# Normalising attention outputs instead of attention weights in the last block of a four-block cross-attention kernel

## The chip, the cores and the metric

The kernel runs on one core of one Trainium2 chip. The metric is the device time of one execution in microseconds; the time of a kernel is the median of several runs. The profile comes from one further execution, taken by the hardware profiler.

## What is computed

Four transformer blocks are applied one after the other to x of shape (8, 112, 256), with a context of shape (8, 375, 192) that all four share. All is float32. Blocks 0 and 1 have self-attention, cross-attention and a gated feed-forward part with 16 heads of 64; block 2 is one cross-attention with heads of 64. Block 3, which the change touches, has 16 heads of 16:

```python
h = _layernorm(x, ln1_w, ln1_b)
q, k, v = split(h @ qkv_w + qkv_b)                    # 16 heads of 16
attn = softmax(where(causal | tgt_mask, -inf, q @ k.T * scale))
x = x + (attn @ v) @ proj_w + proj_b
h = _layernorm(x, ln2_w, ln2_b)
q = h @ q_w + q_b; k = enc @ k_w + k_b; v = enc @ v_w + v_b
attn = softmax(where(enc_mask, -inf, q @ k.T * scale))
x = x + (attn @ v) @ out_w + out_b
h = _layernorm(x, ln3_w, ln3_b)
x = x + gelu(h @ mlp1_w + mlp1_b) @ mlp2_w + mlp2_b
```

A softmax divides each row of exponentials by its sum. The division is by a number for each query and head, so it can be done on the weights or on the product of the weights with v.

## The kernel before

**Stages and tiles.** The ten stages 0 to 9 are self, cross, feed-forward for blocks 0 and 1, one cross for block 2, and self (7), cross (8), feed-forward (9) for block 3. The 896 rows of x lie in seven tiles of 128 rows. The attention outputs of a stage go to `oT`, which holds channels on the partitions and all rows along the free dimension. In block 3 every head's 16 channels are padded to 32, so that four heads fill 128 partitions and the 16 heads fill four chunks of `oT`.

**Steps.** An attention stage is cut into steps (`add_step`). In stage 7 a step is one batch with all 16 heads in two blocks of eight; in stage 8 it is a quarter of a batch, four heads in two blocks of two. Each step has three parts:

- S (`emit_s`): the score matmuls (L818), then `softmax` for each block: on DVE the mask (L777, stage 7 only), the negated maximum (L783) and a guard for fully masked rows (L787); on ACT one exponential for each head, which also accumulates the sum (L793); then the division. With more than one chunk of keys (stage 8, 375 keys) each head has a reciprocal on DVE (L799) and a multiply on POOL (L800); with one chunk (stage 7, 112 keys) a block has one reciprocal (L803) and one multiply (L804).
- T (`emit_t`): TensorE transposes of the weights into a PSUM tile (L837) and a copy to SBUF (`wT`).
- PV (`emit_pv`): the matmuls of the values with `wT` (L857) and a copy to `oT`.

PSUM copies go through `evac`, which picks ACT (L303, L299) or DVE (L311, L307) by an estimate of each engine's load. The four `mm` PSUM tiles serve all but the scores; the scores have two tiles of their own.

**Around the steps.** The output products of a stage (`add_products`, L549) take, for each of the seven row tiles, a few matmuls of `oT` with the output weights, add to x on DVE (L553), and start the next LayerNorm (`norm`): statistics on DVE (L498, L500, L502), then on POOL a power (L504), the normalised tile xn (L506) and the bias row added to x (L507). `add_norm_transposes` turns xn by TensorE (L520) into `hT`. The values of block 3 are made in `add_self_values` (L605) and `add_context_values` (L728) and spread by `spread_values` (a POOL memset, L624, and a DVE add of the bias row, L625). Two constant tiles `rvs` hold those bias rows.

**What sets the order.** TensorE's order is the order in which the program is emitted. A planner (`Plan`) emits it: in each round the score part of step i+2, the PV part of step i, and the T parts of step i+1, with filler items between (projections, keys, values, products, transposes). An item has a cost in us, a deadline counted in steps, the keys that it needs, and for each of these a gap that must have passed in the planner's own time. `ready` takes the item with the earliest deadline among those whose gaps are over; `pace` spreads fillers over the steps up to their deadlines. The other engines' orders are chosen by the scheduler of the framework and are in-order once chosen. The weights come through a ring of seven slots on SP's DMA queue (`add_load`).

Of the kernel before, what the change touches and what calls it, by code (L numbers as in the profile page):

```python
# [17 lines left out]
H = 16  # L18
# [44 lines left out]
def last_batch(t):  # L63
    return min(B - 1, (P * (t + 1) - 1) // T)
# [198 lines left out]
def kernel(ctx: ExitStack, tc: tile.TileContext, a: dict, out: bass.AP):  # L263
# [19 lines left out]
        return ps_m.tile([P, 512], F32, tag="mm", name="mm")  # L283

    plan = Plan(RINGS)
    load = {"act": 0.0, "dve": 0.0}

    def busy(eng, us):
        load[eng] = max(load[eng], plan.now) + us
# [68 lines left out]
    ctxA = const.tile([KA, B * S], F32, name="ctxA")  # L358
    ctxB = const.tile([2 * KB, B * S], F32, name="ctxB")
    cmask = const.tile([T, B, T], F32, name="cmask")  # L360
    rvs = [const.tile([P, D], F32, name=f"rv{i}") for i in range(2)]

    got = {}

# [74 lines left out]
    def add_ctx_narrow(key, name):  # L439


        def fn():
            t = wpool.tile([P, 2, D], F32, tag="w", name=name)
            nc.gpsimd.memset(t[KB : KB + 1, 1, :], 0.0)
            nc.sync.dma_start(t[:, 0, :], a[name][0:KA, :])
            nc.sync.dma_start(t[:KB, 1, :], a[name][KA:DC, :])
            got[key] = t

        plan.add_load(Item(("load", key), 0, fn, makes=[key]))
# [144 lines left out]

            plan.add(Item(key, 1.5, fn, deadline(j, u), uses=[w], makes=[key], deps=h_deps(st, lo, hi), seg=SEG[st]))

    def add_self_values(st, b, w, deadline, wide, bias=None):
        for hf in range(2 if wide else 1):
            key = ("v", st, b, hf, 0)

            def fn(hf=hf, key=key):
                ps = mm_tile()
                n = 512 if wide else D
                for k in range(2):
                    nc.tensor.matmul(  # L605
                        ps[:T, :n], lhsT=hT[:, k, b * T : (b + 1) * T],
                        rhs=got[w][:, k, hf * 512 : hf * 512 + n], start=(k == 0), stop=(k == 1),
                    )
                t = vpool.tile([P, 512], F32, tag="v", name="v")
                if wide:  # L610
                    evac(t[:T, :], ps[:T, :], n)
                else:
                    spread_values(t, ps, T, bias)
                got[key] = t

            plan.add(
                Item(key, 1.75 if wide else 0.9, fn, deadline(b, hf), uses=[w], makes=[key],
                     deps=h_deps(st, b * T, (b + 1) * T), seg=SEG[st])
            )
# [98 lines left out]
    def ctx_deps(b):  # L718
        return [(("ctxT", b), 4.0)]

    def add_context_values(st, b, w, deadline, bias):
        for c, (k0, kl) in enumerate(KCH):
            key = ("v", st, b, 0, c)

            def fn(k0=k0, kl=kl, key=key):
                ps = mm_tile()
                for k, (ct, rows) in enumerate(((ctxA, KA), (ctxB, KB + 1))):
                    nc.tensor.matmul(  # L728
                        ps[:kl, :D], lhsT=ct[:rows, b * S + k0 : b * S + k0 + kl],
                        rhs=got[w][:rows, k, :], start=(k == 0), stop=(k == 1),  # L730
                    )
                t = vpool.tile([P, 512], F32, tag="v", name="v")
                spread_values(t, ps, kl, bias)
                got[key] = t

            plan.add(Item(key, 0.9, fn, deadline(b), uses=[w], makes=[key],
                          deps=ctx_deps(b) + [(("put", 0), 5.0)], seg=SEG[st]))
# [20 lines left out]


    steps = []  # L760

    def add_step(st, b, blocks, dh, nk, qs, ks, qap, kap, vtile, masked, guard, opos, ochunk):

# [8 lines left out]
        def softmax(blk, ps):  # L772
            ns = len(blk) // 2
            sv = ps[:, :, : ns * nk].rearrange("p b (s k) -> p b s k", k=nk)
            pr = ppool.tile([T, 2, ns, nk], F32, tag="pr", name="pr")
            if masked:
                nc.vector.tensor_add(  # L777
                    pr, sv, cmask[:, b, :].unsqueeze(1).unsqueeze(1).to_broadcast([T, 2, ns, nk])
                )
                sv = pr  # L780
                busy("dve", 1.1)
            nm = small.tile([T, 2, 4], F32, tag="nm", name="nm")
            nc.vector.tensor_reduce(nm[:, :, :ns], sv, AX.X, ALU.max, negate=True)  # L783
            busy("dve", 0.16 + 0.00104 * 2 * ns * nk)
            if guard:

                nc.vector.tensor_scalar_min(nm[:, :, :ns], nm[:, :, :ns], -0.01 * NEG)  # L787
                busy("dve", 0.16)
            sums = small.tile([T, 2, 4], F32, tag="sums", name="sums")
            rinv = small.tile([T, 2, 4], F32, tag="rinv", name="rinv")  # L790
            for n in range(len(blk)):
                bk, sl = n % 2, n // 2
                nc.scalar.activation(  # L793
                    pr[:, bk, sl, :], sv[:, bk, sl, :], AF.Exp, bias=nm[:, bk, sl : sl + 1],
                    accum_out=sums[:, bk, sl : sl + 1],
                )
                busy("act", 0.46 + 0.00084 * nk)
                if nch > 1:
                    nc.vector.reciprocal(rinv[:, bk, sl : sl + 1], sums[:, bk, sl : sl + 1])  # L799
                    nc.gpsimd.tensor_scalar_mul(pr[:, bk, sl, :], pr[:, bk, sl, :], rinv[:, bk, sl : sl + 1])  # L800
                    busy("dve", 0.16)
            if nch == 1:
                nc.vector.reciprocal(rinv[:, :, :ns], sums[:, :, :ns])  # L803
                nc.gpsimd.tensor_tensor(  # L804
                    pr, pr, rinv[:, :, :ns].unsqueeze(3).to_broadcast([T, 2, ns, nk]), ALU.mult
                )
                busy("dve", 0.16)
            return pr

        def emit_s():  # L810
            tiles = [ps_s.tile([T, 2, 512], F32, tag="s", name="s") for _ in blocks]

            order = [(i, n) for i, blk in enumerate(blocks) for n in range(len(blk))]
            if dh == 16:
                order.sort(key=lambda e: (e[1] // 2, e[0]))
            for i, n in order:
                h = blocks[i][n]
                nc.tensor.matmul(  # L818
                    tiles[i][:, n % 2, (n // 2) * nk : (n // 2 + 1) * nk], lhsT=qap(h), rhs=kap(h),
                    start=True, stop=True,  # L820
                )
            for i, blk in enumerate(blocks):
                pr = softmax(blk, tiles[i])
                for n, h in enumerate(blk):
                    cell[h] = pr[:, n % 2, n // 2, :]
# [52 lines left out]
                 deps=[(("T", s, i), 0) for i in range(len(banks))]), False  # L878
        )
        steps.append(len(banks))  # L880

    def self_steps(st, dh):
        first = len(steps)
# [64 lines left out]
    def after_pv(first, per):  # L948

        return lambda t: [(("PV", first + per * (last_batch(t) + 1) - 1), 1.2)]  # L950

    def q_deadline(first, per, j):
        return first + per * 2 * j - 3.4

# [9 lines left out]


    info = []
    SEG = [0, 0, 0, 1, 1, 1, 2, 2, 2, 2]
    for kind, dh in (
        ("self", 64), ("cross", 64), ("ff", 0), ("self", 64), ("cross", 64), ("ff", 0),
        ("cross", 64), ("self", 16), ("cross", 16), ("ff", 0),  # L970
# [21 lines left out]
    def self_stage(st, names, wq, wk, wv, wo):  # L992
# [7 lines left out]
            add_pair_projection(st, "k", j, wk, us, dl, None,  # L1000
                                (lambda m: bcols[:, 8 + m : 9 + m]) if L3 else None)
        for b in range(B):
            add_self_values(st, b, wv, lambda b, hf: first + per * b + hf - 1.3, not L3, rvs[0])

    def cross_stage(st, wq, wk, wv, qscale, vscale):
        kind, first, per, dh = info[st]
# [4 lines left out]
        for b in range(B):  # L1011
            if L3:
                add_context_keys(st, b, wk, 4, lambda b, m: first + 4 * b + m - 3.2, lambda m: bcols[:, 12 + m : 13 + m])
                add_context_values(st, b, wv, lambda b: first + 4 * b - 1.3, rvs[1])
            else:

                add_key_jobs(st, b, wk, lambda b, u: first + 4 * b + u - 3.0)
                add_value_jobs(st, b, wv, lambda b, i: first + 4 * b + (0, 0, 2)[i] - 1.5 + 0.1 * i, vscale)
# [42 lines left out]
    def w(name):  # L1061
        return ("w", name)
# [53 lines left out]
    add_masks()  # L1116
    L3 = "L3_xattn_"

    def add_rvs():
        def fn():  # L1120
            nc.sync.dma_start(rvs[0], a["v_row"].to_broadcast([P, D]))
            r = ROWS.index(L3 + "v_b")
            nc.sync.dma_start(rvs[1], a["rows"][r : r + 1, :].to_broadcast([P, D]))

        plan.add_load(Item(("load", "rvs"), 0, fn))

    add_rvs()
    add_padded(w("q3"), L3 + "qkv_w", slice(0, D))
    add_padded(w("k3"), L3 + "qkv_w", slice(D, 2 * D))
    add_w(w("v3"), L3 + "qkv_w", slice(2 * D, 3 * D))  # L1130
    add_row(("row", 7), L3 + "proj_b")
    add_padded_rows(w("o3"), L3 + "proj_w")
    add_padded(w("qc"), L3 + "q_w", None)
# [11 lines left out]
    add_products(6, 7, w(L + "Wo"), 8, after_pv(f6, 4), norm_by(7))  # L1145
    add_norm_transposes(7, L3 + "ln1_w", L3 + "ln1_b", hT_by(7))
    self_stage(7, None, w("q3"), w("k3"), w("v3"), w("o3"))
    add_products(7, 8, w("o3"), 4, after_pv(f7, 1), norm_by(8))
    add_norm_transposes(8, L3 + "ln2_w", L3 + "ln2_b", hT_by(8))
    cross_stage(8, w("qc"), w("kc"), w("vc"), 0.25, None)  # L1150
    add_products(8, 9, w("oc"), 4, after_pv(f8, 4), norm_by(9))
    add_norm_transposes(9, L3 + "ln3_w", L3 + "ln3_b", hT_by(9))
    ff_stage(9, None, w("m1"), L3 + "mlp1_b", AF.Gelu, f9 - 1)
    add_products(9, None, w("m2"), 8, after_ff(9), lambda t: f9 + 1 + 0.1 * t)
# [74 lines left out]
```

## Time and profile before

| what | value |
|---|---|
| median of 3 runs | 1757.38 us (1756.21 to 1757.7) |
| profiled execution | 1756.8 us, of which 1755.0 us are the span from first to last instruction |
| mean granted TensorE clock | 0.995 |
| PE busy | 1696.6 us |
| POOL busy | 906.6 us |
| DVE busy | 874.6 us |
| ACT busy | 756.1 us |
| block 3: stage 7 from about | 1400 us |
| block 3: stage 8 | from about 1480 to 1702 us |
| block 3: feed-forward, last output | to 1755 us |

PE is the matrix unit of TensorE, PEld its weight loads, DVE the vector engine, ACT the scalar engine, POOL the GpSimd engine. In a row of a group, `x128 | 155.8, 1235` means 128 instructions, 155.8 us busy in all, 1235 ns each; behind the next bar stands the idle time of the engine just ahead of them, and who ended it. A matmul's mean overlaps with its neighbours', so that its cost in a row is the busy time divided by the count. In the table of stretches, the two columns behind the engines are the granted TensorE clock and the DMA engines' busy share.

### The profile page before, as it was taken

To read this page: it belongs to the slowest core of one execution; us is meant where nothing else is said; L and a number is where in the kernel's file an instruction comes from. 1 tells how busy PE (TensorE), PEld (TensorE's weight loads), DVE (VectorE), ACT (ScalarE), POOL (GpSimd) and SP (SyncE) were. 2 spreads that over 40 slices of the span, in tenths; PEclk is the share of its full clock that TensorE was granted. 3 is DMA by queue.
4 is the path that set the end of the run, shared out by engine and by line. 5 is a ranking of instruction groups with operands and counts; after the bars stand their busy time and mean duration, and the time that the engine had idled before them with its cause. 6 is when DMAs were issued, how large, how long until landed. Compare 5 with 4: busy or idle time off the path is not lost.

```text
span 1755.0 us, 30348 instructions
## 1 busy us (share of the span) xinstructions
PE 1696.6 (97%) x11886; PEld 1186.7 (68%) x11886; DVE 874.6 (50%) x2046; ACT 756.1 (43%) x2410; POOL 906.6 (52%) x825
## 2 busy tenths in 40 slices
PE   5999999999999999999999999999999998999989
PEld 4877766666658887666666656666666876666656
DVE  1454454555522444554555522445555588666740
ACT  2553443444521544434444431444444366555641
POOL 4223455566702322655466612645566845888880
PEclk9999999999999999999999999999999999999999
DMA  5011011000101101000000101100000101000000
GB/s 176 11 48 53 3 29 54 25 1 1 49 27 43 28 10 40 25 28 1 25 1 1 43 28 9 10 1 1 7 1 7 12 9 55 1 1 2 1 1 22
DMA packets 39464, 39.12 MB, mean 22 GB/s; under 512 B 16928, under 2 KB 34568, under 8 KB 39321
## 3 DMA queue, kind: packets, MB, share of 16 engines
q1 hardware_dynamic: 39257, 37.13, 7.6%
q8 instruction: 94, 1.54, 0.4%
q14 instruction: 49, 0.40, 0.1%
q0 software_dynamic: 64, 0.05, 0.0%
HBM read 35.48 MB, written 0.92 MB: 21 GB/s over the span
## 4 chain that ended last, share of the span: by engine, by line
PE 85%; POOL 6%; ACT 4%; DVE 4%; issue 1%; DMA 0%; SPq 0%; ACTq 0%; POOLq 0%; DVEq 0%
PE mm L581 11%; PE mm L549 11%; PE mm L837 9%; PE s L818 9%; PE mm L857 9%; PE mm L677 7%; PE mm L643 7%; PE mm L1030 7%; PE mm L686 4%; PE mm L652 4%; POOL pr L800 4%; PE mm L605 3%; ACT pr L793 3%; DVE nm L783 2%; POOL xn L506 1%; PE mm L728 1%
## 5 line engine op out<-in xcount | busy, mean ns | idle before, releaser
L800 POOL TENSOR_SCALAR pr<-pr,rinv 112x375 f32<-112x375 f32 x512 | 623.5, 1236 | 366.2 <-DVE rinv L799 362.8
L793 ACT ACTIVATE pr<-s,nm 112x375 f32<-112x375 f32 (+1 forms) x768 | 373.5, 501 | 240.4 <-DVE nm L783 166.6
L783 DVE TENSOR_REDUCE nm<-s 112x2 f32<-112x750 f32 (+1 forms) x288 | 266.2, 953 | 68.3 <-PE s L818 63.9
L837 PE MATMUL mm<-ident,pr 112*128 112x112 f32 (+2 forms) x1920 | 241.3, 265 | 13.1 <-POOL pr L800 5.2
L837 PEld LDWEIGHTS mm<-ident,pr 112*128 112x128 f32 (+2 forms) x1920 | 214.5, 152 | 58.3 <-issue 15.5
L303 ACT COPY wT<-mm 128x448 f32<-128x448 f32 (+2 forms) x285 | 150.1, 534 | 190.5 <-PE mm L837 190.2
L857 PEld LDWEIGHTS mm<-wT,v 128*64 128x64 f32 (+5 forms) x3840 | 160.3, 129 | 84.6 <-issue 32.5
L804 POOL TENSOR_TENSOR pr<-pr,rinv 112x896 f32<-112x896 f32 x48 | 80.8, 1683 | 253.7 <-DVE rinv L803 228.1
L818 PE MATMUL s<-kT,qT 64*112 64x375 f32 (+3 forms) x1792 | 207.6, 392 | 0.0
L857 PE MATMUL mm<-wT,v 128*64 128x112 f32 (+5 forms) x3840 | 200.1, 264 | 7.4 <-ACT wT L303 4.5
L818 PEld LDWEIGHTS s<-kT,qT 64*112 64x112 f32 (+1 forms) x1792 | 113.1, 172 | 68.2 <-issue 15.3
L793 ACT ACTIVATION_READ_ACCUMULATOR pr<-s,nm 112x1 f32 x768 | 158.0, 206 | 0.0
L799 DVE RECIPROCAL rinv<-sums 112x1 f32<-112x1 f32 x512 | 83.4, 163 | 98.7 <-ACT pr L793 88.1
L311 DVE COPY kT<-mm 128x375 f32<-128x375 f32 (+1 forms) x117 | 65.5, 560 | 133.4 <-PE mm L652 114.4
L311 DVE COPY wT<-mm 128x448 f32<-128x448 f32 (+2 forms) x195 | 118.6, 612 | 21.3 <-PE mm L837 18.2
L311 DVE COPY v<-mm 128x512 f32<-128x512 f32 (+2 forms) x75 | 51.8, 691 | 141.2 <-PE mm L686 118.7
L303 ACT COPY kT<-mm 128x375 f32<-128x375 f32 (+1 forms) x107 | 51.1, 478 | 129.0 <-PE mm L652 115.3
L504 POOL TENSOR_TENSOR rs<-ve,mhalf 128x1 f32<-128x1 f32 x70 | 39.4, 564 | 126.1 <-DVE ve L502 123.9
L553 DVE TENSOR_TENSOR x<-mm,x 128x256 f32<-128x256 f32 x70 | 29.5, 422 | 143.2 <-PE mm L549 143.1
L643 PE MATMUL mm<-ctxA,L_xattn_Wk 128*128 128x375 f32 x256 | 91.5, 480 | 0.0
L677 PE MATMUL mm<-L_xattn_Wv,ctxA 128*128 128x512 f32 (+1 forms) x192 | 90.7, 595 | 0.4 <-ACT hT L299 0.4
L506 POOL TENSOR_SCALAR xn<-x,mv,rs 128x256 f32<-128x256 f32 x70 | 85.8, 1226 | 7.7 <-PE mm L520 1.1
(130 smaller groups left out, 2349.4 us busy)
## 6 DMA issues: line engine op xcount, KB each, us to landing
L_xattn_Wq<-in_L_xattn_Wq_dram SPq DMA_DIRECT2D x3, 1024.0 KB, 6.7
L_xattn_Wo<-in_L_xattn_Wo_dram SPq DMA_DIRECT2D x3, 1024.0 KB, 15.9
L_xattn_w_ff<-in_L_xattn_w_ff_dram SPq DMA_DIRECT2D x3, 1024.0 KB, 5.6
L_xattn_Wp<-in_L_xattn_Wp_dram SPq DMA_DIRECT2D x2, 1024.0 KB, 7.5
L_xattn_wq<-in_L_xattn_wq_dram SPq DMA_DIRECT2D x2, 1024.0 KB, 5.0
L_xattn_wo<-in_L_xattn_wo_dram SPq DMA_DIRECT2D x2, 1024.0 KB, 5.7
L_xattn_mlp_w<-in_L_xattn_mlp_w_dram SPq DMA_DIRECT2D x2, 1024.0 KB, 4.9
cn<-in_ctx_dram SPq DMA_DIRECT2D x2, 843.8 KB
```

The lines of the kernel that those rows point to most:

```text
L303: nc.scalar.copy(dst, src)
L311: nc.vector.tensor_copy(dst, src)
L549: nc.tensor.matmul(ps[:, :D], lhsT=oT[:, c, t * P : (t + 1) * P], rhs=got[w][:, c, :], start=(c == 0), stop=(c == n - 1),)
L581: nc.tensor.matmul(ps[:, i * 2 * T : (i + 1) * 2 * T], lhsT=got[w][:, k, m * P : (m + 1) * P], rhs=hT[:, k, lo:hi], start=(k == 0), stop=( ...
L643: nc.tensor.matmul(ps[:, :S], lhsT=got[w][:, (2 * u + i) * P : (2 * u + i + 1) * P], rhs=ctxA[:, cols], start=True, stop=False,)
L677: nc.tensor.matmul(ps[: KCH[c][1], :], lhsT=lhs(ctxA, slice(0, KA), c), rhs=got[w][:, hf * 512 : (hf + 1) * 512], start=True, stop=False,)
L783: nc.vector.tensor_reduce(nm[:, :, :ns], sv, AX.X, ALU.max, negate=True)
L793: nc.scalar.activation(pr[:, bk, sl, :], sv[:, bk, sl, :], AF.Exp, bias=nm[:, bk, sl : sl + 1], accum_out=sums[:, bk, sl : sl + 1],)
L800: nc.gpsimd.tensor_scalar_mul(pr[:, bk, sl, :], pr[:, bk, sl, :], rinv[:, bk, sl : sl + 1])
L818: nc.tensor.matmul(tiles[i][:, n % 2, (n // 2) * nk : (n // 2 + 1) * nk], lhsT=qap(h), rhs=kap(h), start=True, stop=True,)
L837: nc.tensor.transpose(pt[:kl, i * T : (i + 1) * T], cell[h][:, c * P : c * P + kl], ident[:T, :T])
L857: nc.tensor.matmul(po[p0 : p0 + dp, blk * T : (blk + 1) * T], lhsT=got[vk][:kl, hv * dp : (hv + 1) * dp], rhs=wt, start=(c == 0), stop=(c ...
```

## The change

In stages 7 and 8 (`dh == 16`) the weights stay unnormalised: `softmax` returns after the exponentials, whose sums go into one tile `bsums` for each batch, a column for each head. After a batch's last step two planner items are added. The first, R, inverts the sums on the queries' partitions and spreads each reciprocal over its head's 32 padded columns in a constant tile `rb` (POOL). The second, N, turns the four chunks of `rb` by TensorE, copies them to SBUF, and multiplies that batch's columns of `oT` in place (POOL). The output products of the two stages depend on N instead of PV. The two constant bias tiles `rvs` are dropped, and each bias row becomes a third row of its value weights' tile. Blocks 0 to 2 keep their code.

```diff
+    rb = const.tile([T, H, 32], F32, name="rb")
-    rvs = [const.tile([P, D], F32, name=f"rv{i}") for i in range(2)]
...
         def fn():
-            t = wpool.tile([P, 2, D], F32, tag="w", name=name)
+            t = wpool.tile([P, 3, D], F32, tag="w", name=name)
             nc.gpsimd.memset(t[KB : KB + 1, 1, :], 0.0)
             nc.sync.dma_start(t[:, 0, :], a[name][0:KA, :])
             nc.sync.dma_start(t[:KB, 1, :], a[name][KA:DC, :])
+            r = ROWS.index("L3_xattn_v_b")
+            nc.sync.dma_start(t[:, 2, :], a["rows"][r : r + 1, :].to_broadcast([P, D]))
+            got[key] = t
...
+    def add_self_narrow(key, name, cols):
+        def fn():
+            t = wpool.tile([P, 3, D], F32, tag="w", name=name)
+            nc.sync.dma_start(t[:, 0:2, :], a[name][:, cols].rearrange("(c p) n -> p c n", p=P))
+            nc.sync.dma_start(t[:, 2, :], a["v_row"].to_broadcast([P, D]))
             got[key] = t
...
-                    spread_values(t, ps, T, bias)
+                    spread_values(t, ps, T, got[w][:, 2, :])
...
+            if dh == 16:
+
+                for n, h in enumerate(blk):
+                    bk, sl = n % 2, n // 2
+                    nc.scalar.activation(
+                        pr[:, bk, sl, :], sv[:, bk, sl, :], AF.Exp, bias=nm[:, bk, sl : sl + 1],
+                        accum_out=bsums[(st, b)][:, h : h + 1],
+                    )
+                    busy("act", 0.46 + 0.00084 * nk)
+                return pr
             sums = small.tile([T, 2, 4], F32, tag="sums", name="sums")
...
         def emit_s():
+            if dh == 16 and (st, b) not in bsums:
+                bsums[(st, b)] = small.tile([T, H], F32, tag="bsums", name="bsums")
...
+        if dh == 16 and ochunk + len(heads) * dp // P == 4:
+
+            def emit_norm():
+
+                rs = small.tile([T, H], F32, tag="rsum", name="rsum")
+                nc.vector.reciprocal(rs, bsums.pop((st, b)))
+                nc.gpsimd.tensor_copy(rb, rs.unsqueeze(2).to_broadcast([T, H, 32]))
+
+            def emit_scale():
+                rf = rb.rearrange("p h d -> p (h d)")
+                ps = mm_tile()
+                for c in range(4):
+                    nc.tensor.transpose(ps[:, c * T : (c + 1) * T], rf[:, c * P : (c + 1) * P], ident[:T, :T])
+                rt = tpool.tile([P, 448], F32, tag="wT", name="rT")
+                evac(rt, ps[:, : 4 * T], 4 * T)
+                cols = slice(b * T, (b + 1) * T)
+                nc.gpsimd.tensor_tensor(
+                    oT[:, 0:4, cols], oT[:, 0:4, cols], rt.rearrange("p (c t) -> p c t", t=T), ALU.mult
+                )
+
+            prev = [] if b == 0 else [(("N", st, b - 1), 0)]
+            plan.add(Item(("R", st, b), 0, emit_norm, s + 0.4, deps=[(("S", s), 4.0)] + prev, seg=SEG[st]))
+            plan.add(
+                Item(("N", st, b), 0.4, emit_scale, s + 0.9, deps=[(("R", st, b), 2.0), (("PV", s), 1.2)], seg=SEG[st])
+            )
...
+    def after_norm(st):
+        return lambda t: [(("N", st, last_batch(t)), 2.5)]
...
-    add_rvs()
...
-    add_w(w("v3"), L3 + "qkv_w", slice(2 * D, 3 * D))
+    add_self_narrow(w("v3"), L3 + "qkv_w", slice(2 * D, 3 * D))
...
-    add_products(7, 8, w("o3"), 4, after_pv(f7, 1), norm_by(8))
+    add_products(7, 8, w("o3"), 4, after_norm(7), norm_by(8))
...
-    add_products(8, 9, w("oc"), 4, after_pv(f8, 4), norm_by(9))
+    add_products(8, 9, w("oc"), 4, after_norm(8), norm_by(9))
```

More of the change, by code (lines that the diff above doesn't have):

```diff
@@ L285 @@
     plan = Plan(RINGS)
+    SEG = [0, 0, 0, 1, 1, 1, 2, 2, 2, 2]
     load = {"act": 0.0, "dve": 0.0}
@@ L446, in fn @@
             nc.sync.dma_start(t[:KB, 1, :], a[name][KA:DC, :])
+            r = ROWS.index("L3_xattn_v_b")
+            nc.sync.dma_start(t[:, 2, :], a["rows"][r : r + 1, :].to_broadcast([P, D]))
+            got[key] = t
+        plan.add_load(Item(("load", key), 0, fn, makes=[key]))
+    def add_self_narrow(key, name, cols):
[3 more added lines that the diff above has]
+            nc.sync.dma_start(t[:, 2, :], a["v_row"].to_broadcast([P, D]))
             got[key] = t
@@ L595, in add_pair_projection, with add_self_values @@
             plan.add(Item(key, 1.5, fn, deadline(j, u), uses=[w], makes=[key], deps=h_deps(st, lo, hi), seg=SEG[st]))
-    def add_self_values(st, b, w, deadline, wide, bias=None):
+    def add_self_values(st, b, w, deadline, wide):
         for hf in range(2 if wide else 1):
@@ L719, in ctx_deps, with add_context_values @@
         return [(("ctxT", b), 4.0)]
-    def add_context_values(st, b, w, deadline, bias):
+    def add_context_values(st, b, w, deadline):
         for c, (k0, kl) in enumerate(KCH):
@@ L732, in fn @@
                 t = vpool.tile([P, 512], F32, tag="v", name="v")
-                spread_values(t, ps, kl, bias)
+                spread_values(t, ps, kl, got[w][:, 2, :])
                 got[key] = t
@@ L760 @@
     steps = []
+    bsums = {}
     def add_step(st, b, blocks, dh, nk, qs, ks, qap, kap, vtile, masked, guard, opos, ochunk):
@@ L966 @@
     info = []
-    SEG = [0, 0, 0, 1, 1, 1, 2, 2, 2, 2]
     for kind, dh in (
@@ L1002, in self_stage @@
         for b in range(B):
-            add_self_values(st, b, wv, lambda b, hf: first + per * b + hf - 1.3, not L3, rvs[0])
+            add_self_values(st, b, wv, lambda b, hf: first + per * b + hf - 1.3, not L3)
     def cross_stage(st, wq, wk, wv, qscale, vscale):
@@ L1013, in cross_stage @@
                 add_context_keys(st, b, wk, 4, lambda b, m: first + 4 * b + m - 3.2, lambda m: bcols[:, 12 + m : 13 + m])
-                add_context_values(st, b, wv, lambda b: first + 4 * b - 1.3, rvs[1])
+                add_context_values(st, b, wv, lambda b: first + 4 * b - 1.3)
             else:
@@ L1117 @@
     L3 = "L3_xattn_"
[L1119 to L1125, printed above, removed]
-    add_rvs()
     add_padded(w("q3"), L3 + "qkv_w", slice(0, D))
     add_padded(w("k3"), L3 + "qkv_w", slice(D, 2 * D))
-    add_w(w("v3"), L3 + "qkv_w", slice(2 * D, 3 * D))
+    add_self_narrow(w("v3"), L3 + "qkv_w", slice(2 * D, 3 * D))
     add_row(("row", 7), L3 + "proj_b")
```

## Prediction

> **What bounds the kernel now.** I read the page's busy table and slices first, to find the engine that is full; then the busy time by stretch over the last block, where the change lies; then PE's own waits there; then the rows of the operations that go and come; last the timeline around the longest wait.
>
> ```profile
> PE 1696.6 (97%) x11886; PEld 1186.7 (68%) x11886; DVE 874.6 (50%) x2046; ACT 756.1 (43%) x2410; POOL 906.6 (52%) x825
> ...
> PE   5999999999999999999999999999999998999989
> ...
> POOL 4223455566702322655466612645566845888880
> ```
>
> TensorE is busy 97% of the span. Its order is written out by hand, so every microsecond in which it stands and every instruction added to it counts. POOL is the other engine to watch: it reaches 8 tenths only at the end, which is the last block.
>
> ```profile
> 1400.00:1475.00 75.00, 66.64 (x718) 56.56 (x718) 61.10 (x130) 46.70 (x235) 37.34 (x38) 0.98 0.08 24
> 1475.00:1505.00 30.00, 27.42 (x287) 19.82 (x286) 22.16 (x51) 17.80 (x67) 16.70 (x15) 1.00 0.11 36
> 1505.00:1660.00 155.00, 144.91 (x1371) 101.46 (x1370) 107.40 (x304) 90.46 (x270) 136.64 (x130) 1.00 0.01 1
> 1660.00:1702.00 42.00, 34.98 (x316) 25.17 (x315) 24.09 (x76) 21.83 (x59) 39.23 (x38) 0.94 0.00 1
> ```
>
> Columns: stretch, length, then busy us of PE, PEld, DVE, ACT, POOL, and the granted clock. The first row is the self-attention of the last block, the others its cross-attention. PE stands 8.4 + 2.6 + 10.1 + 7.0 = 28.1 us there, of the 58 us that it stands in the whole span (1755.0 - 1696.6); nearly 20 us of the rest is the start, before any of this. So the most that can be recovered is 28 us and what the clock loses: 0.98 and 0.94 are three stretches near half clock (1468.4 to 1471.8 at 0.52, 1676.6 to 1680.0 at 0.51, 1700.5 to 1704.0 at 0.53), each costing about 1.7 us. POOL is busy 88% of the third row and 93% of the fourth.
>
> ```profile
> PE mm L520 <- POOL xn L506: 5.9, 3, 3.2
> PE mm L837 <- POOL pr L800: 5.2, 8, 0.9
> PE mm L857 <- ACT wT L303: 4.5, 3, 1.7
> PE mm L837 <- ACT kT L299: 4.3, 7, 1.0
> PE mm L857 <- DVE wT L311: 2.8, 1, 2.8
> PE mm L837 <- DVE oT L311: 1.6, 3, 1.0
> PE mm L837 <- ACT wT L303: 1.3, 1, 1.3
> PE mm L520 <- DVE oT L311: 1.0, 1, 1.0
> ```
>
> PE's waits from 1400 to 1702 us (total, times, longest). POOL ends 11.1 us of them: 5.2 are transposes that wait for a normalised weight, 5.9 are LayerNorm transposes whose xn stood in POOL's queue. The other 15.5 us are PSUM copies (wT, kT, oT) that ACT or DVE make late.
>
> **The change, part by part.** *POOL's normalisation goes.*
>
> ```profile
> L800 POOL TENSOR_SCALAR pr<-pr,rinv 112x375 f32<-112x375 f32 x128 | 155.8, 1235 | 21.7 <-DVE rinv L799 18.4 <-DVE nm L787 3.3
> L804 POOL TENSOR_TENSOR pr<-pr,rinv 112x896 f32<-112x896 f32 x16 | 26.9, 1682 | 36.8 <-DVE rinv L803 35.5 <-PE mm L837 1.3
> ```
>
> 155.8 + 26.9 = 182.7 us of POOL in these 302 us. For each of 16 batches (8 in each attention) come a copy of 112x512 and a multiply of 128x448. Neither is in the trace; the adds of L507 (128x256, 725 ns) and L804 (896 elements, 1682 ns) put 1.5 ns on an element, so 1.1 and 1.0 us at most; the memset of L454 (128x1024, 0.95 us) puts the copy at 0.5 us at least. I take 1.1 + 1.0, together 34 us. POOL falls from 230 to some 81 us of the 302. The 5.2 us go whole, since a transpose then waits for the exponential alone. Of the 5.9 us I take 4.9: at 1668.70 four L800 (4.88 us) stand ahead of the pow and xn of the tile that PE waits for.
>
> ```profile
> 1671.91 0.44 PE L520 MATMUL mm<-ident,xn 128*128 128x128 f32 x2
> 1675.53 0.44 PE L520 MATMUL mm<-ident,xn 128*128 128x128 f32 x2 [3.18 <-POOL xn L506]
> 1675.81 2.94 PE L549 MATMUL mm<-L_xattn_out_w,oT 128*128 128x256 f32 x8
> ```
>
> The wait of 3.18 us is followed by half clock: eight L549 take 2.94 us where they take 1.9 elsewhere. The Trainium skill ("TensorE: Matmul & The Clock Gate", Part 1, "What's actually happening") has the clock fall after an idle window of about 3.4 us that runs freely; here a gap just under that did it, and waits of 0.9 us in a row (1694 to 1699) led to the third stretch. Both ends are POOL's, so I count 2 x 1.7 = 3.3 us recovered; taken strictly by the page, shorter gaps need not trip it and the sum would be 3 us smaller. Sum for POOL: 5.2 + 4.9 + 3.3 = 13.4 us.
>
> *DVE's reciprocals go.* 128 of 163 ns and 16 of 200 ns are 24.1 us, and DVE stood 41.6 us in front of them for ACT (32.0 + 9.6), with copies queued behind: at 1455.2 and 1466.5 the last wT copy of stage 7 comes right after such a reciprocal. L787, which releases ACT's next exponential, also comes after them. Added: 16 reciprocals of 112x16, about 0.2 us as the 112x8. So copies come earlier, but ACT's share stays late: its queue holds 16 exponentials of about 0.37 us in a row in stage 7, and the copy behind them waits either way. Of the 15.5 us I take 40%, 6.2 us, and half of the remaining clock stretch, 0.8: 7.0 us. Ends: none and 17.2 us. What is late next is PE itself; in the middle the chain from scores to last exponential is about 5.2 us against a step of 5.9 to 7.8 us, so it sets no step.
>
> *The spreading comes.* Per batch four transposes 112x128, the same shape as L837's, 64 in all, on PE. L837's row of that shape is 37.0 us for 256 in the cross-attention (144 ns each), 131.6 us for 1024 over the whole kernel (129 ns): 8.2 to 9.2 us; I take 9.2, since the step is near that row. The same skill page (Part 4, "PE-mode transpose") speaks against it: about 275 ns each, for bf16 in another kernel, and not counted as activity by the clock. That would be 17.6 us and leave almost no gain. Here twelve in a row took 1.35 us at full clock, so the row decides. Nothing hides this: it is added to the bound engine.
>
> *New waits.* The batch's copies of 128x448 (16 of 0.53 us on ACT or 0.61 on DVE) lie beside PE, as DVE sheds 24 us. The reciprocal waits for a batch's last exponential, 5 us after the scores in stage 8 and 10 to 12 in stage 7, and what stands behind it on DVE is PSUM copies and the next maximum; POOL's copy waits for it with LayerNorm behind. The planner puts the transposes after the batch's PV, two steps on, so they should find rb done. The output products, seven for each attention, now wait for transposes 0.5, copy 0.6, multiply 1.0, that is 2.1 us against a planned gap of 2.5; a LayerNorm group on POOL (0.57 + 1.23 + 0.73 us) or exponentials on ACT ahead of it would make PE wait. Lower end 0 (a gain has no reason), upper end 14 x 1.1 = 15 us; I take 2 us, near the low end, because other fillers usually stand between. The single rb makes one batch wait for the last one's transposes, a whole batch earlier: nothing. The two bias rows move from constants to the value weights' loads: one more SP issue of 0.36 us each, at about 1253 and 1422 us; the first values are made at 1391 and about 1488: nothing, and 1 to 6 us if that lead were gone. At the end, 15 us of first-half feed-forward products cover the last batch's longer way.
>
> **Sum** against the profiled execution's 1756.8 us (span 1755.0 and 1.8 around it): -13.4 - 7.0 + 9.2 + 2.0 = -9.2, so 1747.6; the median of the runs is 0.6 higher, so 1748.
>
> **The rivals.**
> - *PE closes nearly up.* With DVE unblocked all the copies come in time and no new wait appears: 17.2 instead of 7.0, and 0 instead of 2: 1736. For it: DVE's 41.6 us of waiting. Against: three of the copy waits sit on ACT behind exponentials that stay.
> - *Exchange.* The late copies stay as they are, since ACT's exponentials make them late, and the added transposes eat POOL's share: -13.4 + 9.2 + 3 = -1: 1756. This is also the case in which the change does not reach the bound: PE was 93 to 97% busy there anyhow.
> - *The multiply takes the place of the normalisation, and the time ends slower.* The place is the products' head of queue on PE: the copy rT lands behind exponentials on ACT, the POOL multiply behind a LayerNorm group. The gain before new waits is 11.2 us, so it decides from 11.2 / 14 = 0.8 us for each product; at 1.15 us it is 16 us, net +5: 1762. For it: the planned gap leaves only 0.4 us. Against: POOL is then 27% busy.
>
> **How the numbers follow.** Likeliest 1748: 0.52 (1743 to 1753). Nearly closed 1736: 0.20. Exchange 1756: 0.14. Slower 1762: 0.14. About 0.2% (3.5 us) is what a measurement of this kernel can tell from no change, so faster 0.72, same 0.14, slower 0.14. The range 1737 to 1759 leaves out half of the closed case and most of the slower one.
>
> **What would show it.** After: no POOL wait of L837; 64 more transposes of some 0.14 us; POOL at or below 30% over these 302 us; PE standing 10 to 16 us instead of 28 over the last block; full clock at its end. Wrong if products wait for POOL's multiply or the transposes for rb by more than 0.8 us each, if DVE stands at the new reciprocal while wT copies queue behind it, or if the copy waits keep their 15 us.

## The result and the profile after

| kernel | median | runs | ratio to before |
|---|---|---|---|
| before | 1756.22 us | 5 (1756.12 to 1757.7) | 1 |
| changed | 1741.75 us | 5 (1739.21 to 1743.98) | 0.992 (0.9908 to 0.9931) |

14.5 us less, 0.8%. The forecast was 1748, 9.2 us less, in a range of 1737 to 1759. The profiled execution took 1743.63 us, with a span of 1741.8 us (1755.0 before).

The page of the changed kernel, its busy times and slices:

```profile
PE 1696.0 (97%) x11950; PEld 1191.5 (68%) x11950; DVE 871.4 (50%) x1946; ACT 751.0 (43%) x2398; POOL 752.8 (43%) x713
...
PE   5999999999999999999999999999999998999999
...
POOL 4213455465712313554556621745466833122130
```

POOL loses 154 us, and its full stretch at the end is gone. PE is as busy as before with 64 instructions more; what fell is the time in which it stands, from 58.4 to 45.8 us. That is 12.6 of the 13.2 us by which the span became shorter. By stretch, with the columns as before (cross-attention now ends at about 1690 us, not 1702):

```profile
1400.00:1475.00 75.00, 64.37 (x719) 54.47 (x718) 60.05 (x122) 43.34 (x214) 23.15 (x35) 1.00 0.09 25
1475.00:1505.00 30.00, 27.83 (x266) 21.68 (x268) 20.67 (x41) 19.28 (x81) 6.63 (x10) 0.89 0.12 36
1505.00:1660.00 155.00, 154.12 (x1471) 111.22 (x1472) 109.80 (x244) 91.21 (x274) 28.65 (x45) 1.00 0.01 1
1660.00:1690.00 30.00, 28.70 (x304) 21.21 (x303) 21.40 (x55) 18.01 (x49) 16.99 (x21) 1.00 0.01 2
```

In the middle of the cross-attention PE stands 0.9 us of 155 where it stood 10.1. In the self-attention (first row) it stands 10.6 us where it stood 8.4: that stage got worse. The second row's clock of 0.89 is two stretches of 3.4 us at half clock, from 1475.5 and 1492.6 us, right behind waits of 1.6 and 1.7 us. PE's waits from 1400 to 1690 us, the larger ones:

```profile
PE mm L883 <- ACT wT L304: 4.3, 3, 1.7
PE mm L618 <- DVE oT L312: 2.1, 2, 1.3
PE mm L594 <- ACT hT L300: 1.8, 1, 1.8
PE mm L720 <- DVE oT L312: 1.6, 1, 1.6
PE mm L533 <- DVE nm L801: 1.1, 1, 1.1
...
PE mm L562 <- POOL oT L923: 0.3, 1, 0.3
```

POOL ends 0.3 us of PE's waits, 11.1 before: a product waits once for POOL's new multiply. The kT waits of stage 8 (4.3 us) are gone. New are those of L618, L594 and L720, all in the self-attention or just behind it. They take back most of what went: in the whole view the waits for late PSUM copies are 13.3 us, against 16.5 before. The rows of what was added, on PE over 1400 to 1742 us and on POOL over 1400 to 1690 us:

```profile
L919 PE MATMUL mm<-ident,rb 112*128 112x112 f32 x64 | 9.8, 279 | 0.0
```

```profile
L923 POOL TENSOR_TENSOR oT<-oT,rT 128x448 f32<-128x448 f32 x15 | 17.1, 1140 | 39.4 <-DVE rT L312 33.9 <-ACT rT L304 5.5
L913 POOL COPY rb<-rsum 112x512 f32<-112x512 f32 x16 | 9.8, 610 | 89.4 <-DVE rsum L912 69.0 <-PE mm L741 12.5 <-PE mm L919 5.3
```

The last thing to read is DVE's queue. Before, DVE stood 41.6 us at the reciprocals, which waited for ACT (1400 to 1702 us):

```profile
DVE rinv L799 <- ACT pr L793: 32.0, 80, 0.8
DVE rinv L803 <- ACT pr L793: 9.6, 9, 2.8
```

And ACT in turn waited ahead of stage 8's exponentials, before and after (1484 to 1700 us):

```profile
L793 ACT ACTIVATE pr<-s,nm 112x375 f32<-112x375 f32 x128 | 72.3, 570 | 72.6 <-DVE nm L787 69.3 <-PE mm L837 2.6 <-POOL rs L504 0.8
```

```profile
L807 ACT ACTIVATE pr<-s,nm 112x375 f32<-112x375 f32 x128 | 71.7, 570 | 59.1 <-DVE nm L801 53.6 <-PE mm L533 3.5 <-PE mm L919 1.5
```

The exponential waits 15.7 us less for DVE's guarded maximum, because that no longer queues behind reciprocals that wait for ACT: in the same window the wait is 67.3 us where the multiplies alone are taken away (before_no_mult below) and 57.8 where the reciprocals are (before_no_recip).

Something else moved with the reciprocals. Each had added 0.16 us to the estimate of DVE's load by which `evac` picks an engine (`busy("dve", 0.16)`), and the new path adds nothing for its few. So more copies go to DVE. The copies of stage 8's keys on ACT, before and after (1484 to 1700 us):

```profile
L299 ACT ACTIVATE kT<-mm,bcols 128x375 f32<-128x375 f32 x16 | 8.7, 575 | 0.7 <-PE mm L707 0.7
```

```profile
L300 ACT ACTIVATE kT<-mm,bcols 128x375 f32<-128x375 f32 x6 | 3.5, 578 | 0.5 <-PE mm L720 0.3
```

### The profile page after: what moved, and what is told of

It reads as the page before. It is cut to its first block, busy times and chain, and to the rows that moved or that the text cites. A ratio compares the mean times of both kernels' runs of the same rounds, so it can differ in the third digit from the quotient of the medians.

```text
span 1741.8 us, 30272 instructions
## 1 busy us (share of the span) xinstructions
PE 1696.0 (97%) x11950; PEld 1191.5 (68%) x11950; DVE 871.4 (50%) x1946; ACT 751.0 (43%) x2398; POOL 752.8 (43%) x713
## 4 chain that ended last, share of the span: by engine, by line
PE 90%; DVE 3%; ACT 3%; POOL 2%; issue 1%; DMA 0%; SPq 0%; ACTq 0%; POOLq 0%; DVEq 0%
PE mm L562 12%; PE mm L594 11%; PE mm L863 10%; PE s L844 10%; PE mm L883 9%; PE mm L690 7%; PE mm L1083 7%; PE mm L656 7%; PE mm L699 4%; PE mm L665 4%; PE mm L618 3%; PE mm L720 2%; ACT pr L807 2%; PE mm L741 1%; DVE nm L797 1%; DVE pr L791 1%
## 5 line engine op out<-in xcount | busy, mean ns | idle before, releaser
L824 POOL TENSOR_SCALAR pr<-pr,rinv 112x375 f32<-112x375 f32 x384 | 467.6, 1236 | 344.6 <-DVE rinv L823 344.5
L817 ACT ACTIVATE pr<-s,nm 112x375 f32<-112x375 f32 (+1 forms) x640 | 301.2, 488 | 167.7 <-DVE nm L797 166.5
L863 PE MATMUL mm<-ident,pr 112*128 112x112 f32 (+2 forms) x1920 | 237.3, 264 | 2.0 <-ACT hT L300 0.9
L828 POOL TENSOR_TENSOR pr<-pr,rinv 112x896 f32<-112x896 f32 x32 | 53.8, 1682 | 216.9 <-DVE rinv L827 192.6
L817 ACT ACTIVATION_READ_ACCUMULATOR pr<-s,nm 112x1 f32 x640 | 132.8, 208 | 0.0
L807 ACT ACTIVATE pr<-s,nm 112x375 f32<-112x375 f32 x128 | 71.7, 570 | 59.1 <-DVE nm L801 53.6
L823 DVE RECIPROCAL rinv<-sums 112x1 f32<-112x1 f32 x384 | 62.5, 163 | 65.5 <-ACT pr L817 56.1
```

What stands on the lines that cost most here:

```text
L817: nc.scalar.activation(pr[:, bk, sl, :], sv[:, bk, sl, :], AF.Exp, bias=nm[:, bk, sl : sl + 1], accum_out=sums[:, bk, sl : sl + 1],)
L863: nc.tensor.transpose(pt[:kl, i * T : (i + 1) * T], cell[h][:, c * P : c * P + kl], ident[:T, :T])
```

## The experiments

Theory at the outset: the gain is POOL's freed queue, less the added transposes. Rivals: it is DVE's freed queue; or the price of the spreading is not its TensorE time. Twelve kernels follow, each timed four or five times beside the kernel before (medians of 1755.9 to 1756.8 us).

**Nothing spread (no_scale).**

```diff
-        if dh == 16 and ochunk + len(heads) * dp // P == 4:
+        if False:
...
-    add_products(7, 8, w("o3"), 4, after_norm(7), norm_by(8))
+    add_products(7, 8, w("o3"), 4, after_pv(f7, 1), norm_by(8))
```

(and the same for stage 8's products.)

> The changed kernel without R and N: no inverted sums, no spreading transposes, no multiply of the output, so the last block's attention stays undivided; the products depend on PV again. Theory (the spreading costs its TensorE time and nothing else): 64 transposes of 0.153 us are 9.8 us, so 1741.75 - 9.8 = 1732. Rival (the waits for rb, for the copy and for POOL's multiply cost as much again): 1724 or less. Rival (they lie in time in which TensorE stood anyway): 1739 or more.

Measured 1724.99 us (ratio 0.9825, 0.9812 to 0.9839). The spreading costs 16.8 us. That is just outside the second case (1724 or less) and 7 us from the theory: clearly more than 9.8 us of transposes. What is recovered in all is 31.7 us.

**POOL's multiplies alone taken away (before_no_mult).** The kernel before, all its reciprocals kept.

```diff
-                    nc.gpsimd.tensor_scalar_mul(pr[:, bk, sl, :], pr[:, bk, sl, :], rinv[:, bk, sl : sl + 1])
+                    if dh != 16:
+                        nc.gpsimd.tensor_scalar_mul(pr[:, bk, sl, :], pr[:, bk, sl, :], rinv[:, bk, sl : sl + 1])
```

(and the same guard for stage 7's multiply.)

> The kernel before, with POOL's multiplies of the last block left out (the attention there stays undivided) and all its reciprocals on DVE kept. Theory (POOL's queue is the cause, and DVE's reciprocals a small part): of the 24 us that the change recovers in all (14.5 us of gain and 9.8 us of added transposes) about 18 come, so 1738. Rival (the reciprocals that hold up DVE are the larger part): 1746 to 1750.

Measured 1740.08 us (0.9906, 0.9893 to 0.992): 16.6 us. POOL brings about what the theory said, but only half of the 31.7. PE's waits of this kernel from 1400 to 1686 us:

```profile
PE mm L859 <- ACT wT L303: 4.5, 3, 1.7
PE mm L839 <- ACT kT L299: 3.4, 6, 0.8
PE mm L859 <- DVE wT L311: 2.8, 1, 2.8
PE mm L839 <- DVE oT L311: 1.5, 3, 0.9
```

POOL's are gone; the late copies stand as they did before.

**The reciprocals alone taken away (before_no_recip).** The kernel before with a constant in place of `rinv`, in block 3 only.

```diff
-                    nc.vector.reciprocal(rinv[:, bk, sl : sl + 1], sums[:, bk, sl : sl + 1])
-                    nc.gpsimd.tensor_scalar_mul(pr[:, bk, sl, :], pr[:, bk, sl, :], rinv[:, bk, sl : sl + 1])
+                    if dh != 16:
+                        nc.vector.reciprocal(rinv[:, bk, sl : sl + 1], sums[:, bk, sl : sl + 1])
+                        busy("dve", 0.16)
+                    rv = halfs if dh == 16 else rinv
+                    nc.gpsimd.tensor_scalar_mul(pr[:, bk, sl, :], pr[:, bk, sl, :], rv[:, bk, sl : sl + 1])
```

(and the same for stage 7's. The estimate of DVE's load falls here as it does in the change.)

> The kernel before without the last block's reciprocals on DVE; POOL multiplies by a constant 0.5 instead, so the attention there stays undivided. Taking the multiplies away brought 16.6 us and the reciprocals then another 15.1. Theory (two causes side by side, DVE's queue being one of its own): the reciprocals alone bring 8 to 15 us, 1741 to 1748. Rival (POOL's multiply bounds the steps while it is there): 1751 to 1757.

Measured 1748.29 us (0.9952, 0.9939 to 0.9964): 7.8 us, just outside what the theory gave and clear of the rival. So the reciprocals are a cause of their own. Behind the multiplies' removal they are worth 15.1 us (1740.08 to 1724.99), with them in place 7.8. Most of the difference is the clock, by the estimate below. The five runs here were granted 0.990 to 0.994, those of the kernel before beside it 0.995 to 0.996, and a thousandth of a span is 1.7 us. In the trace, two stretches at half clock follow waits of 1.3 us for POOL's xn, at 1517.9 and 1569.1 us:

```profile
1518.80:1525.60 6.80, 6.80 (x46) 4.38 (x45) 3.45 (x8) 1.94 (x5) 5.59 (x8) 0.50 0.01 2
1570.00:1576.80 6.80, 6.80 (x46) 4.39 (x45) 3.46 (x8) 1.94 (x5) 5.58 (x8) 0.50 0.00 0
```

An estimate, with the share of the span that each run's clock lost taken off it: the reciprocals bring some 14 us with the multiplies in place and some 12 without. The two causes then about add up.

What these runs don't separate is how the reciprocals cost their time. Two things go with the reciprocals: DVE's standing at them, and the estimate that kept copies on ACT. Over 1484 to 1700 us ACT makes 16 of stage 8's key copies with the reciprocals (before, before_no_mult) and 4 to 6 without (before_no_recip, no_scale, changed). In stage 7 `evac` chose nearly the same engines (13 of 36 wT copies on ACT, then 11), and the reciprocals' removal still shortened it by over 5 us (table below), 1.7 of them one stretch at half clock less; so there the freed queue is the likelier way. In stage 8 the two can't be told apart. A kernel without the reciprocals but with their 0.16 us kept in the estimate would tell; none was run. In no_scale PE's waits from 1400 to 1669 us are these:

```profile
PE mm L883 <- ACT wT L304: 3.6, 3, 1.4
PE mm L533 <- DVE nm L801: 1.1, 1, 1.1
PE mm L720 <- DVE oT L312: 0.8, 1, 0.8
PE mm L863 <- ACT hT L300: 0.8, 2, 0.5
PE mm L863 <- DVE oT L312: 0.8, 2, 0.5
```

Of the larger copy waits only ACT's wT in stage 7 stays, the one that sits behind a row of exponentials.

**One stage at a time (only_cross, only_self).** The scheme, its planner items and the products' dependence in one stage only.

```diff
-            if dh == 16:
+            if st == 8:
...
-        if dh == 16 and ochunk + len(heads) * dp // P == 4:
+        if st == 8 and ochunk + len(heads) * dp // P == 4:
```

> The new scheme in the cross-attention (stage 8) alone; stage 7 divides its weights as before. Theory: in the traces the first scores of stage 8 start 4.0 us later after the change than before it (1488.6 against 1484.6), so stage 7 loses and stage 8 gains all: 1741.75 - 4 = 1738. Rival (stage 7 gains too by its freed reciprocals and the later start is a stretch of half clock that fell there): 1742 to 1748.

> The new scheme in the self-attention (stage 7) alone; stage 8 divides its weights as before. Theory: 32 transposes are 4.9 us of TensorE and little POOL waiting goes there, so it is slower than before: 1756 + 3 to 4 = 1760. Rival (DVE's blocked reciprocals were what made stage 7's copies late): 1750 to 1754.

Measured 1736.97 us (0.989, 0.9876 to 0.9903) and 1764.12 us (1.0044, 1.0032 to 1.0057). As the theory had it, the edit gains 19.7 us in the cross-attention alone and loses 7.4 in the self-attention alone, twice what was expected. only_cross is 4.8 us faster than the changed kernel and the fastest here that leaves nothing out. only_self's waits from 1395 to 1500 us hold the three new ones of the changed kernel, with the same 2.1, 1.8 and 1.6 us.

Where each kernel's time lies can be read from its profiled execution: from stage 7's first score to its last PV, and from there to stage 8's last PV, with the granted clock. These are single executions, and a stretch at half clock more or less is 1.7 us.

| kernel | stage 7, us (clock) | stage 8, us (clock) |
|---|---|---|
| before | 95.5 (0.98) | 205.8 (0.99) |
| before_no_mult | 95.3 (0.98) | 191.2 (1.00) |
| before_no_recip | 90.3 (1.00) | 202.9 (0.96) |
| no_scale | 89.4 (1.00) | 181.7 (1.00) |
| no_trans | 92.7 (1.00) | 185.5 (1.00) |
| tile_only | 96.9 (0.96) | 185.2 (1.00) |
| changed | 100.2 (0.97) | 188.4 (1.00) |
| only_self | 100.2 (0.97) | 210.6 (0.98) |

(no_trans and tile_only follow below.) The multiplies' removal acts in stage 8 alone. The reciprocals' acts in both. The spreading costs 10.8 us in stage 7 and 6.7 in stage 8. Of what only_self lost, about half lies in stage 8, which there divides its weights as before and ran in part at a lower clock. The loss inside stage 7 is 4.7 us.

**The transposes twice (twice).**

```diff
-                for c in range(4):
+                for c in list(range(4)) * 2:
```

> The changed kernel with each of its 64 spreading transposes made twice; the output is the same. Theory (TensorE is the bound, a transpose costs its 0.153 us): 1741.75 + 9.8 = 1751.5. Rival (they also push the chain to POOL's multiply and the products): 1756 or more. Rival (partly hidden in waits): 1747 or less.

Measured 1742.51 us (0.9921, 0.9908 to 0.9935), 0.8 us more than the changed kernel. The theory, 9.8 us more, falls: a further transpose doesn't cost 0.153 us. Their row shows one part, over 1400 to 1702 us:

```profile
L919 PE MATMUL mm<-ident,rb 112*128 112x112 f32 x128 | 15.2, 261 | 0.0
```

The second 64 add 5.4 us of busy time, 0.084 us each, where the first took 0.153. So a group's busy time over its count is not what one more of the same costs. The other part is the clock: this kernel's runs were granted 0.998 to 0.999, the changed kernel's 0.996 to 0.999, and a thousandth of a span is 1.7 us. In the profiled executions, from stage 7's last PV to stage 8's last it is 190.6 us against 188.4, both at full clock. The doubling therefore costs some 2 to 4 us, mostly paid back by fewer stretches of half clock in stage 7.

**No transposes at all (no_trans), and one (tile_only).** In no_trans the transposes, their PSUM tile and the copy rT go, and POOL multiplies by a constant; R stays. In tile_only one transpose and a copy of 112 columns stay, with the tile, and its chunk multiplies all four.

```diff
-                for c in range(4):
+                for c in range(1):
...
-                evac(rt, ps[:, : 4 * T], 4 * T)
+                evac(rt[:, :T], ps[:, :T], T)
```

> The changed kernel without the spreading transposes, their PSUM tile and the copy rT; POOL multiplies the output by a constant, R stays, so the attention isn't divided rightly. Leaving R and N out brought 16.7 us, but doubling the transposes cost only 0.8. Theory (transposes and their PSUM tile cost 8 to 10 us, R the rest): 1732 to 1734. Rival (R's place on DVE costs most of it): 1737 or more. Rival (transposes, tile and copy are all of it): 1727 or less.

> The changed kernel with one spreading transpose for each batch instead of four, a copy of 112 columns instead of 448, and the same PSUM tile; all four chunks of the output are multiplied by that one chunk, so three quarters of the division are wrong. Leaving transposes, tile and copy out brought 11.4 us (1730.4), doubling the transposes cost 0.8. Theory (the price is the extra tile in the ring of four and the wait for its copy, not TensorE's work): most of it stays, 1737 to 1741. Rival (the transposes and the length of the copy): 1731 to 1734.

Measured 1730.38 us (0.9855, 0.984 to 0.9869) and 1736.41 us (0.9885, 0.9869 to 0.9902). The first lies between two of its cases: transposes, tile and copy are 11.4 us, R and the rest of N 5.4. The second is just outside the theory's 1737 and 2.4 us off its rival: the first transpose with its tile and a short copy is 6.0 us, the other three with 336 columns of copy 5.3. But some 4 of the 6.0 us are the clock, at 1.7 us for a thousandth (0.996 to 0.997 granted in tile_only's runs, 0.998 to 0.999 in no_trans's), and by the table they lie in stage 7; in stage 8 tile_only is no slower than no_trans. There, at full clock, all of transposes, tile and copy cost 2.9 us (185.5 to 188.4). In tile_only's waits from 1400 to 1686 us,

```profile
PE mm L618 <- DVE oT L312: 2.4, 2, 1.3
PE mm L720 <- DVE oT L312: 1.9, 1, 1.9
```

are there as before. In the changed kernel's order the item behind N's transposes is the one that waits; it needs one of the four PSUM tiles, N has just taken one, and the oldest waits for DVE to copy oT. TensorE's timeline (start, us, then the instruction, its idle time and who ended it):

```profile
1437.75 0.55 PE L919 MATMUL mm<-ident,rb 112*128 112x112 f32 x4
1439.58 1.12 PE L618 MATMUL mm<-L_xattn_qkv_w,hT 128*112 128x256 f32 x4 [1.28 <-DVE oT L312]
```

**The reciprocal's place (late_recip, pool_recip).** Late: R is put behind the last step's transposes. On POOL: the sums are inverted by a power of -1 there.

```diff
-            plan.add(Item(("R", st, b), 0, emit_norm, s + 0.4, deps=[(("S", s), 4.0)] + prev, seg=SEG[st]))
+            plan.add(Item(("R", st, b), 0, emit_norm, s + 0.8, deps=[(("T", s, len(banks) - 1), 0)] + prev, seg=SEG[st]))
```

```diff
-                nc.vector.reciprocal(rs, bsums.pop((st, b)))
+                nc.gpsimd.tensor_tensor(rs, bsums.pop((st, b)), mone, ALU.pow)
```

> The changed kernel with R (the sums' reciprocal and the copy to rb) put behind the transposes of the batch's last step instead of 4 us behind its scores, so that DVE meets the reciprocal when the exponentials are done. If DVE's standing there is what makes the spreading dearer than its transposes: 1735 to 1737. If not: 1740 to 1744.

> The changed kernel with the batch's sums inverted on POOL (a power of -1, 112x16) and not on DVE, so that DVE doesn't stand for the last exponential; putting R later in the program had left DVE standing 16.2 us all the same and brought 2.6 us. Theory (DVE standing in front of PSUM copies is the larger part of what the spreading costs beyond its transposes): 1734 to 1737. Rival (the extra PSUM tile of each batch is, in the ring of four): 1740 or more.

Measured 1739.13 us (0.9901, 0.9885 to 0.9916) and 1739.25 us (0.9904, 0.9887 to 0.992): 2.6 and 2.5 us less than the changed kernel, neither case of either expectation. late_recip didn't do what it was for: the scheduler put the reciprocal early all the same, and DVE's wait there barely moved (changed kernel, then late_recip):

```profile
DVE rsum L912 <- ACT pr L807: 15.6, 13, 2.6
```

```profile
DVE rsum L912 <- ACT pr L807: 16.2, 13, 2.6
```

pool_recip takes the wait away, and it is worth no more than 2.5 us. late_recip gained as much with the wait in place, so not even that is shown to come from the wait. DVE standing at the new reciprocal is a smaller part of the price than I had taken it for.

**The same in the cross-attention (cross_pool).** only_cross with the sums inverted on POOL.

> The new scheme in the cross-attention alone (1737.0 with the sums inverted on DVE), with the sums inverted on POOL. Theory: DVE stands 7.3 us there at the eight reciprocals, at most half of it on TensorE's path: 1733 to 1735. Rival (in stage 8 the standing is beside the path): 1736 to 1738.

Measured 1737.57 us (0.9895, 0.988 to 0.991), not to be told from only_cross: the rival holds, in stage 8 that wait lies beside the path.

**DVE's multiply from PSUM (dve_mult).** No copy rT, no POOL multiply.

```diff
-                rt = tpool.tile([P, 448], F32, tag="wT", name="rT")
-                evac(rt, ps[:, : 4 * T], 4 * T)
...
-                nc.gpsimd.tensor_tensor(
-                    oT[:, 0:4, cols], oT[:, 0:4, cols], rt.rearrange("p (c t) -> p c t", t=T), ALU.mult
+                nc.vector.tensor_tensor(
+                    oT[:, 0:4, cols], oT[:, 0:4, cols], ps[:, : 4 * T].rearrange("p (c t) -> p c t", t=T), ALU.mult
```

> The changed kernel with the output multiplied by DVE straight from the transposes' PSUM tile, so that the copy rT and POOL's multiply go. Leaving R and N out brought 16.7 us, 7 more than the transposes. If the 7 us lie in the chain copy, POOL multiply, products: about 1735. If they lie in DVE standing at the sums' reciprocal (15.6 us in the trace after): no change, 1740 to 1743.

Measured 1743.42 us (0.9927, 0.9915 to 0.994): no gain, so the chain copy, POOL multiply, products is not on the path, as the product's single wait of 0.3 us said.

## Why the prediction was right in direction and short in size

- **POOL's share, 13.4 us: right, and somewhat small.** Taking the multiplies away brings 16.6, all in stage 8. Both kinds of wait went as said (11.1 us to 0.3), and the end of the cross-attention runs at full clock (0.94 before). But two stretches of half clock now lie near 1476 and 1493 us.
- **DVE's share, 7.0 us: the cause was right, the size was off by half.** It measured 15.1 us behind the multiplies' removal, which is what the change does. The failed step is the 40% that I took of the copy waits, on the ground that ACT's exponentials make ACT's copies late in any case. That took the copies' engines as fixed. Without the reciprocals `evac` moved most of stage 8's key copies to DVE, and the exponentials themselves waited less for DVE (69.3 us to 53.6), so the kT waits went; which of the two weighed more stays open. Of the copy waits, 15.3 us in before_no_mult, 6.6 stayed in no_scale: 8.7 us went where I took 6.2. That is the smaller part of the miss. The clock brought about 2.4 us more (0.9972 to 0.9986 in the mean of the runs), and in stage 8 PE's busy time for the same matmuls fell from 185.3 to 180.7 us, which the sum had at nothing; what shortened it wasn't traced. The rival "PE closes nearly up", with 17.2 us for this term, came near its size, but not by the copy waits alone.
- **The spreading, 9.2 us for transposes and 2.0 for new waits: 11.2 predicted, 16.8 measured, and put in the wrong place.** The row of 0.153 us was forecast to 6%, but it is no price: one of the second set costs about half of that or less, and in stage 8 the first 32, with tile and copy, cost 2.9 us, 0.09 each. The rest is stage 7, where waits for late copies and the stretches at half clock behind them come with the PSUM tile, and R with the rest of N, 5.4 us. I had looked for the wait at the products and at rb; neither came. Two of my signs of being wrong did come in part: DVE stood 15.6 us at the new reciprocal, though taking that away brought little, and the copy waits kept 13.3 of their 16.5 us, since the spreading makes about as many anew (6.6 us in no_scale).
- **The sum.** -16.6 - 15.1 + 16.8 = -14.9, against 14.5 measured. That is no test: the three are steps from one kernel to the next, and close by construction. The terms were off by 3.2, 8.1 and 5.6 us. The last has the opposite sign, so it is partly luck that the gain was forecast no more than 5.3 us short.
- **Not foreseen: the stages differ in sign.** I costed the two attentions together. Stage 8 has 128 multiplies of 1.24 us for eight spreadings; stage 7 has 16 multiplies of 1.68 us, with POOL 50% busy and not one POOL wait of a weight, for as many spreadings.
- **The other rivals.** The exchange (1756) would have needed DVE's share to stay at nothing. The slower one needed 0.8 us at each product; it was 0.3 us in all. The costs at nothing held: the bias rows' two extra issues on SP (0.46 and 0.58 us, at 1253 and 1423 us) stand well ahead of the first values that use them (1393 and 1495), and no transpose waited for rb. Of the signs named, PE standing 10 to 16 us (15.0) and POOL at or below 30% (26%) came.

What stays open, besides how the reciprocals' gain divides between the freed queue and the moved copies: how the 11.4 us of transposes, tile and copy divide in stage 7. No kernel with a fifth PSUM tile was run.

## What to carry to other kernels

Cost an edit for each stage apart, even where the code is shared: here the same lines, each stage alone, gained 19.7 us in one and lost 7.4 in the other. When an operation goes, cost what queued behind it on its engine as well as its own waits: DVE stood 41.6 us at reciprocals that waited for ACT, with copies and maxima behind them. Ask too which choices of the program rest on the operation that goes, as the copies' engines did here. Before two effects are said to hide each other, compare the clocks of the runs. When an operation is added to a full TensorE, the waits that it makes at the ring of PSUM tiles can cost more than its matmuls, as in stage 7.

## What the runs showed of the hardware

The changed kernel's five runs differ in step with their granted clock: 1739.2 us at 0.999, 1740.8 at 0.998, 1741.8 at 0.997, 1743.6 and 1744.0 at 0.996. The same program falls into more or fewer stretches of half clock (3.4 us each in the trace) from run to run, some 1.7 us apiece, which is as much as several of the effects above. It took no wait of the 3.18 us seen before the change: stretches came right behind waits of 1.3 us (before_no_recip) and of 1.6 and 1.7 us (the changed kernel). Sixty-four more transposes went with a clock of 0.998 to 0.999, against 0.996 to 0.999 without them. So nothing is seen here of the Trainium skill's remark that the clock gate does not count transposes as activity ("TensorE: Matmul & The Clock Gate", Part 4, "PE-mode transpose"); but eight in a row between other matmuls don't test it. A broadcasting copy of 112x512 on POOL takes 0.61 us, little over half of what I had worked out for it from the adds, and the multiply of 128x448 1.14 us.
